# An adapter layer in float32 on one core: the residual rows added by accumulating DMAs, under a new order of steps

## The chip, the cores and the metric

The kernel runs on one core of a Trainium2 chip. The metric is the device time of one execution in microseconds (us); the time of a version is the median of its runs. Besides, one execution is recorded by the profiler. Its span is the time from the first to the last instruction.

## The reference

For each of 64 samples, x is 64 channels by 1024. The kernel computes a grouped convolution with a context term, then a dense layer with low-rank terms, and adds x itself at the end:

```python
out = conv1d(x, weight, groups=4, K=9, pad=4) + (c @ c_weight.T)[:, :, None] + bias[None, :, None]
A_eff = einsum('bn,nri->bri', gate, lora_A);  B_eff = einsum('bn,nor->bor', gate, lora_B)
y = out @ kernel + ffn_bias
y += B_eff (A_eff out)  +  lora_B_shared (lora_A_shared out)     # per batch of 8 samples
return x + y                                                     # float32, 64 x 64 x 1024
```

## The kernel before

The work is split into 16 "pairs" of four samples (256 rows of 1024). For each pair p there are four groups g of channels, and four output blocks b of 128 x 512: b = 2 * half of the rows + half of the columns. All products are made of float32 values split into a high and a low part (steps named ...hi and ...lo), with three matmuls in place of one.

*Convolution.* `xload` brings a group of x. From pair 3 on, `xohi`/`xolo` split its odd columns and `convo` multiplies them into PSUM; `evmid` moves that to SBUF with the context term added, either on ScalarE ("a", four activations) or on VectorE ("v", one addition). `xdiff` forms differences of columns, `xdhi`/`xdlo` split them, `convd` multiplies them, `evac` adds both parts, and `turned` transposes the result on VectorE. In the first three pairs `xhi`, `xlo` and `conv` do this directly.

*Dense layer.* From pair 1 on, a scheme with 7 products in place of 8 is used: `asum` (GpSimd) forms sums of input blocks, `yhi`/`ylo` split them, and `prod p j` is 12 matmuls into one of the accumulators a, d, c, b. Pair 0 uses `plain`. `keep p j` copies an accumulator to SBUF on ScalarE, `xsum` adds the accumulator b to the first copy (call the result X), `ysum` adds two further copies (call it Y). `lora`, `axlow`, `axsum`, `axhi`, `axlo` make the low-rank factor, and `delta p b` adds its product and the bias to the accumulator of block b.

*End of a block.* `rload p b` brings the 128 x 512 rows of x into a buffer r (SyncE's DMA queue; there are four such buffers). `radd` adds X to it for blocks 1, 2 and 3, `yadd` adds Y for block 3, `total` adds the accumulator on VectorE, and `store` writes r out from ScalarE's DMA queue:

```python
    def radd(p, b, eng="p"):
        r = res[p, b]
        engs[eng].tensor_tensor(r, r, cop[p, "x"], ALU.add)
```

In the opening, weights (`wload`) are loaded, the shared low-rank term is folded into them (`fmm`, `fadd`), they are combined (`wsum`) and split (`whi`, `wlo`), and the gated factors are made by `lload`, `mix`, `mixout`, `mixput` and read back by `aload` and `bload`. `busy` are matmuls on constants ahead of any data.

*Order.* A long string, ORDER, lists every step with its arguments; a last letter names the engine where there is a choice (v VectorE, p GpSimd, a ScalarE). The steps are emitted in this order, and each engine and each DMA queue runs its instructions in the order of emission, since a dependency without a semaphore ties each instruction to the one before it on its engine. The string was written ahead of time; nothing is planned at run time. A buffer of a pool is given out when the step that makes it is emitted, and waits for the last use of the buffer's former content.

Of the kernel before, what the change touches and what calls it, by code (L numbers as in the profile page):

```python
# [10 lines left out]
ALU = mybir.AluOpType  # L11
# [39 lines left out]
small 1, warm, twload 1, busy 29, twload 0, cwload, gload, ctload, cwide, cmul, thi 2, small 0, thi 0, tlo 0 v,  # L51
xload 0 0, xhi 0 0, tlo 2 p, xload 0 1, xlo 0 0 v, conv 0 0, twsum v, xhi 0 1, xlo 0 1 v, conv 0 1, sbload 1,
sbhi 1, csum, evac 0 0 v, turned 0 0, xload 0 2, xhi 0 2, xload 0 3, saload 0, sblo 1 p, xlo 0 2 p, evac 0 1 v,
turned 0 1, saload 1, gmask, xhi 0 3, conv 0 2, xlo 0 3 p, sahi 1, conv 0 3, sahi 0, salo 0 v, fmm 0 1,
sbload 0, sbhi 0, fmm 1 1, wload 1 0, evac 0 2 a, xload 1 0, sblo 0 v, fmm 1 0, salo 1 v, xload 1 1, xhi 1 0,
xhi 1 1, xlo 1 1 p, xlo 1 0 v, turned 0 2, yhi 0 0, ylo 0 0 p, wload 0 1, fadd 0 1, evac 0 3 a, fadd 1 0,
conv 1 0, whi 7 0, fmm 4 0, turned 0 3, xload 1 2, xhi 1 2, wlo 7 0 v, fmm 3 0, wload 1 1, conv 1 1, fadd 1 1,
wload 4 0, fmm 0 0, whi 0 1, wload 0 0, fadd 0 0, evac 1 0 a, plain 0 1 0, fadd 4 0, xlo 1 2 p, turned 1 0,
whi 0 0, wlo 0 1 p, fmm 2 1, fmm 2 0, yhi 0 7, evac 1 1 a, conv 1 2, fmm 5 0, wload 2 1, wload 2 0, fadd 2 0,
wlo 0 0 p, plain 0 0 0, xload 1 3, fadd 2 1, wload 5 0, xhi 1 3, fmm 4 1, xlo 1 3 p, plain 0 0 1, whi 0 2,  # L60
ylo 0 7 v, fadd 5 0, plain 0 3 0, whi 7 1, yhi 0 4, wload 3 0, fadd 3 0, whi 0 3, wload 5 1, fmm 3 1, conv 1 3,
turned 1 1, wlo 7 1 v, wload 3 1, xload 2 0, plain 0 1 1, fadd 3 1, whi 7 2, evac 1 2 v, wlo 7 2 p, wload 4 1,
wlo 0 3 p, wlo 0 2 v, lload 0 6, plain 0 2 0, whi 7 3, plain 0 3 1, fadd 4 1, wload 7 1, turned 1 2, whi 1 1,
plain 0 1 2, lload 0 7, xhi 2 0, plain 0 0 2, ylo 0 4 v, plain 0 3 2, xlo 2 0 v, plain 0 2 1, fmm 5 1,
evac 1 3 a, xload 3 0, wlo 7 3 v, plain 0 2 2, turned 1 3, whi 1 0, yhi 0 1, ylo 0 1 v, fadd 5 1, whi 6 1,
conv 2 0, wload 7 0, thi 1, xdiff 3 0 0 v, wload 6 0, evac 2 0 a, lload 1 5, wlo 1 0 p, fmm 7 0, fadd 7 0,
plain 0 2 3, plain 0 0 3, fmm 6 0, lload 0 2, plain 0 3 3, plain 0 1 3, fadd 6 0, lload 0 5, whi 6 0, asum 1 2,
yhi 1 2, lload 0 0, yhi 1 0, plain 0 0 4, plain 0 2 4, wsum 2 2 v, whi 2 2, lload 1 1, wlo 1 1 p, plain 0 0 5,
fmm 6 1, tlo 1 v, plain 0 2 5, rload 0 2, wlo 6 0 v, wsum 2 1 v, wsum 2 3 v, whi 1 2, wlo 1 2 v, plain 0 1 4,
whi 2 1, asum 1 3, whi 1 3, wlo 1 3 p, xload 2 2, wload 6 1, fadd 6 1, xload 2 1, whi 6 2, lload 0 1, xhi 2 2,  # L70
plain 0 3 4, lload 0 4, plain 0 2 6, lload 1 0, lload 0 3, wsum 2 0 v, fmm 7 1, plain 0 2 7, xload 2 3,
plain 0 0 6, fadd 7 1, whi 6 3, total 0 2, lload 1 6, mix 0 0, mixout 0 0 a, wlo 6 2 v, xhi 2 1, wlo 6 3 v,
wlo 6 1 v, wsum 3 2 v, xlo 2 2 v, mix 0 3, mixout 0 3 a, mix 0 2, mixout 0 2 a, wsum 3 0 v, wsum 5 0 v,
mixput 0 0, whi 2 3, mix 0 1, wsum 3 1 v, mix 1 0, mixput 0 3, mixout 0 1 a, xdiff 3 0 1 p, wsum 4 0 v,
conv 2 2, wlo 2 2 v, whi 2 0, wlo 2 0 v, ylo 1 2 v, plain 0 1 5, wsum 5 1 v, rload 0 0, wsum 5 2 v, wsum 4 2 v,
xlo 2 1 v, plain 0 0 7, mixput 0 1, ylo 1 0 p, mixput 0 2, wlo 2 1 v, prod 1 0, plain 0 1 6, wsum 3 3 v,
wsum 5 3 v, rload 0 1, plain 0 3 5, wsum 4 3 v, bihi, whi 3 2, keep 1 0, plain 0 1 7, lload 1 3, wsum 4 1 v,
plain 0 3 6, mixout 1 0 a, lload 1 7, mix 1 3, aload 0, whi 5 3, yhi 1 3, rload 0 3, lload 1 2, ylo 1 3 v,
mixout 1 3 a, total 0 1, lora 0, mix 1 1, turned 2 0, lora 1, whi 5 0, bilo, xohi 3 0, lload 1 4, mix 1 2,
whi 4 2, wlo 4 2 v, mixout 1 1 a, xolo 3 0 v, whi 3 0, wlo 3 0 v, wlo 3 2 v, yhi 1 1, ylo 1 1 v, mixout 1 2 a,  # L80
asum 1 5, total 0 0, whi 4 1, conv 2 1, axlow 1, axsum 1, xload 3 2, wlo 4 1 p, wlo 2 3 v, whi 4 0,
plain 0 3 7, axlow 0, axsum 0, mixput 1 0, mixput 1 3, wlo 4 0 v, xhi 2 3, xlo 2 3 v, wlo 5 3 v, axhi 1,
prod 1 1, biput 0, axlo 1, whi 3 3, asum 1 6, yhi 1 6, wlo 3 3 v, mixput 1 1, evac 2 1 a, turned 2 1, aload 1,
mixput 1 2, total 0 3, evac 2 2 v, turned 2 2, bload 0 0, whi 3 1, axhi 0, prod 1 2, keep 1 2, conv 2 3,
bhi 0 0, biput 1, yhi 2 0, evac 2 3 a, blo 0 0 v, axlo 0, yhi 1 4, bload 0 1, wlo 3 1 p, prod 1 3, ylo 2 0 v,
delta 0 0 1, total 0 0 1, bhi 0 1, blo 0 1 v, ylo 1 6 p, prod 1 6, whi 4 3, delta 0 3 1, wlo 4 3 v, store 0 0,
ylo 1 4 p, turned 2 3, delta 0 2 1, total 0 3 1, xdhi 3 0, convo 3 0, yhi 1 5, whi 5 1, ylo 1 5 v, xdlo 3 0 v,
delta 1 0, total 0 2 1, xload 3 1, keep 1 3, prod 1 4, evmid 3 0 a, store 0 3, xohi 3 1, xdiff 3 1 0 v,
xdiff 3 1 1 p, wlo 5 1 p, delta 0 1 1, total 0 1 1, wlo 5 0 v, xolo 3 1 p, convd 3 0, evac 3 0, turned 3 0,
asum 2 3, rload 1 0, convo 3 1, yhi 2 1, xdhi 3 1, xdlo 3 1 v, prod 2 0, whi 5 2, store 0 2, delta 1 2,  # L90
xload 3 3, keep 2 0, wlo 5 2 p, yhi 2 3, prod 1 5, total 1 0, xohi 3 3, xolo 3 3 v, asum 2 2, xdiff 3 2 0 p,
store 1 0, convo 3 3, evmid 3 1 a, xdiff 3 2 1 p, convd 3 1, ylo 2 3 v, prod 2 3, rload 1 3, delta 1 1,
ylo 2 1 v, xsum 1, asum 2 5, prod 2 1, xdhi 3 2, evac 3 1, turned 3 1, rload 1 2, radd 1 2 v, xdlo 3 2 v,
xdiff 3 3 0 v, delta 1 3, xohi 3 2, xdiff 3 3 1 p, yhi 2 5, xolo 3 2 v, ylo 2 5 p, yhi 2 2, ylo 2 2 v,
evmid 3 3 a, radd 1 3 v, convo 3 2, total 1 2, store 0 1, evmid 3 2 a, convd 3 2, xdhi 3 3, xdlo 3 3 v,
rload 1 1, radd 1 1 v, bload 1 0, lora 2, axlow 2, asum 2 6, prod 2 2, total 1 1, convd 3 3, evac 3 2,
turned 3 2, axsum 2, xload 4 0, xohi 4 0, xolo 4 0 p, bhi 1 0, yhi 2 4, ylo 2 4 v, axhi 2, prod 2 5, keep 2 3,
yhi 3 0, ysum 1 p, xdiff 4 0 0 v, xdiff 4 0 1 v, prod 2 4, store 1 1, xload 4 1, xohi 4 1, xolo 4 1 p,
yadd 1 v, blo 1 0 v, xdhi 4 0, axlo 2, delta 2 0, yhi 2 6, evac 3 3, keep 2 2, xdlo 4 0 v, convo 4 0,
turned 3 3, convd 4 0, rload 2 0, evmid 4 0 a, total 1 3, total 2 0, ylo 3 0 v, lora 3, xdiff 4 1 0 v,  # L100
xdiff 4 1 1 p, asum 3 3, yhi 3 3, prod 3 0, convo 4 1, ylo 3 3 v, evac 4 0, turned 4 0, xdhi 4 1, xload 4 3,
xohi 4 3, xdlo 4 1 v, asum 3 2, xolo 4 3 v, yhi 3 2, ylo 2 6 v, xload 4 2, xdiff 4 2 0 p, store 1 2,
xdiff 4 2 1 p, xohi 4 2, prod 3 3, yhi 3 1, bload 1 1, evmid 4 1 a, delta 2 2, ylo 3 2 v, xolo 4 2 v, asum 3 5,
store 2 0, convd 4 1, xdhi 4 2, xsum 2, convo 4 2, evmid 4 2 a, evac 4 1, xdlo 4 2 v, rload 2 2, radd 2 2 p,
total 2 2, xdiff 4 3 0 v, xdiff 4 3 1 p, prod 2 6, turned 4 1, yhi 3 4, bhi 1 1, convd 4 2, evac 4 2, keep 3 0,
prod 3 2, ylo 3 1 v, rload 2 3, radd 2 3 v, ysum 2 v, convo 4 3, yadd 2 v, xdhi 4 3, xdlo 4 3 v, ylo 3 4 v,
aload 2, prod 3 1, convd 4 3, turned 4 2, blo 1 1 p, xload 5 0, yhi 3 5, xohi 5 0, keep 3 2, asum 3 6,
keep 3 3, xload 5 1, xohi 5 1, delta 2 3, prod 3 4, delta 2 1, xdiff 5 0 0 p, xdiff 5 0 1 v, axlow 3,
ylo 3 5 p, evmid 4 3 a, total 2 3, prod 3 5, store 2 3, xolo 5 0 p, rload 2 1, yhi 3 6, radd 2 1 p, rload 3 0,
axsum 3, evac 4 3, axhi 3, turned 4 3, yhi 4 0, axlo 3, delta 3 0, xload 5 2, xdhi 5 0, store 1 3, xdlo 5 0 v,  # L110
convd 5 0, convo 5 0, ylo 3 6 v, bload 2 0, ylo 4 0 v, xdiff 5 1 0 v, xdiff 5 1 1 p, total 2 1, prod 3 6,
evmid 5 0 a, prod 4 0, asum 4 3, yhi 4 3, evac 5 0, xsum 3, yhi 4 4, ylo 4 3 p, delta 3 3, delta 3 2,
total 3 0, ylo 4 4 v, lora 4, xolo 5 1 p, xdhi 5 1, xdlo 5 1 v, store 3 0, yhi 4 1, ylo 4 1 v, xohi 5 2,
convo 5 1, keep 4 0, bhi 2 0, prod 4 1, rload 3 3, asum 4 2, yhi 4 2, radd 3 3 v, turned 5 0, xdiff 5 2 0 p,
ysum 3 v, evmid 5 1 a, xdiff 5 2 1 v, ylo 4 2 v, delta 3 1, xolo 5 2 p, rload 3 1, radd 3 1 p, blo 2 0 v,
# [702 lines left out]
```

## Time and profile before

| | us |
|---|---|
| median of three runs | 448.88 |
| lowest and highest run | 448.42, 450.63 |
| profiled execution | 447.48 |
| its span | 445.7 |
| TensorE (PE) busy | 438.3 |
| VectorE (DVE) busy | 391.3 |
| ScalarE (ACT) busy | 251.2 |
| GpSimd (POOL) busy | 234.5 |

The profile's page lists each engine's busy time as a share of the span. A group of instructions is given by line, engine, operation, and tiles as out<-in; then come the busy time, the mean nanoseconds of one, and the idle time of the engine just before them with what ended it. SP is SyncE, and a "q" behind an engine's name means its DMA or instruction queue. DMA moved 67.05 MB; SyncE's queue took 38.9% of the DMA engines' time and ScalarE's 10.2%.

### The profile page before, as it was taken

To read this page: it belongs to the slowest core of one execution; us is meant where nothing else is said; L and a number is where in the kernel's file an instruction comes from. 1 tells how busy PE (TensorE), PEld (TensorE's weight loads), DVE (VectorE), ACT (ScalarE), POOL (GpSimd) and SP (SyncE) were. 2 spreads that over 40 slices of the span, in tenths; PEclk is the share of its full clock that TensorE was granted. 3 is DMA by queue.
4 is the path that set the end of the run, shared out by engine and by line. 5 is a ranking of instruction groups with operands and counts; after the bars stand their busy time and mean duration, and the time that the engine had idled before them with its cause. 6 is when DMAs were issued, how large, how long until landed. Compare 5 with 4: busy or idle time off the path is not lost.

```text
span 445.7 us, 7717 instructions
## 1 busy us (share of the span) xinstructions
PE 438.3 (98%) x2557; PEld 358.7 (80%) x2557; DVE 391.3 (88%) x615; ACT 251.2 (56%) x639; POOL 234.5 (53%) x202
## 2 busy tenths in 40 slices
PE   8999999999999999999999999999999999999996
PEld 7677658888888888888878888888888888888884
DVE  5998979899899899889899899899798989887783
ACT  5877468556655566446555655646554745654440
POOL 3766024754747653555444445464656475467543
PEclk9999999999999999999999999999999999999999
DMA  8999582461625463534345453443536354262243
GB/s 229 300 280 308 147 251 66 142 186 49 186 82 158 136 190 110 170 120 136 97 139 147 151 182 91 119 142 90 175 98 186 95 169 151 72 222 90 91 150 118
DMA packets 52488, 67.05 MB, mean 150 GB/s; under 512 B 6112, under 2 KB 34016, under 8 KB 52448
## 3 DMA queue, kind: packets, MB, share of 16 engines
q1 hardware_dynamic: 42512, 49.83, 38.9%
q10 hardware_dynamic: 9936, 16.73, 10.2%
q8 instruction: 20, 0.33, 0.3%
q14 instruction: 20, 0.16, 0.1%
HBM read 47.65 MB, written 18.87 MB: 149 GB/s over the span
## 4 chain that ended last, share of the span: by engine, by line
PE 91%; DMA 4%; DVE 2%; issue 1%; SPq 0%; ACT 0%; ACTq 0%; DVEq 0%
PE mm_a L592 19%; PE mm_d L592 18%; PE mm_c L592 17%; PE mm_b L592 9%; PE cv L346 8%; PE cm L346 4%; PE axp L602 3%; PE cv L318 2%; DMA wr<-in_dram 2%; PE mx L528 2%; PE mm_a L580 1%; PE mm_c L580 1%; DMA ls<-in_dram 1%; DMA ctt<-in_dram 1%; PE mm_d L580 1%; PE mm_a L660 1%
## 5 line engine op out<-in xcount | busy, mean ns | idle before, releaser
L592 PE MATMUL mm_a<-wh,y 128*128 128x512 f32 x240 | 79.6, 392 | 0.0
L592 PE MATMUL mm_d<-wh,y 128*128 128x512 f32 x240 | 79.2, 391 | 0.0
L592 PE MATMUL mm_c<-wh,y 128*128 128x512 f32 x240 | 79.1, 391 | 0.0
L364 ACT ACTIVATE md<-cm,cadd 128x64 f32<-128x64 f32 x208 | 48.2, 315 | 44.8 <-PE cm L346 41.1
L326 POOL TENSOR_TENSOR xf<-xt 128x256 f32<-128x256 f32 x45 | 33.3, 747 | 49.4 <-DVE xd L270 39.4
L265 ACT CAST xd<-xf 128x512 fp32r<-128x512 f32 x52 | 32.5, 626 | 44.9 <-PE cv L346 20.7
L265 ACT CAST y<-s 128x512 fp32r<-128x512 f32 x60 | 37.2, 624 | 30.5 <-POOL s L412 15.3
L592 PEld LDWEIGHTS mm_a<-wh,y 128*128 128x128 f32 x240 | 45.1, 188 | 9.9 <-issue 0.4
L592 PEld LDWEIGHTS mm_d<-wh,y 128*128 128x128 f32 x240 | 45.1, 188 | 9.2 <-issue 0.2
L592 PEld LDWEIGHTS mm_c<-wh,y 128*128 128x128 f32 x240 | 45.1, 188 | 9.1 <-ACT c L636 0.2
L387 DVE STREAM_TRANSPOSE z<-v 128x512 f32<-128x512 f32 x64 | 45.4, 709 | 3.2 <-PE axp L602 1.9
L592 PE MATMUL mm_a<-wl,y 128*128 128x512 f32 x120 | 46.9, 391 | 0.0
L592 PE MATMUL mm_c<-wl,y 128*128 128x512 f32 x120 | 46.8, 390 | 0.0
L592 PE MATMUL mm_d<-wl,y 128*128 128x512 f32 x120 | 46.8, 390 | 0.0
L346 PE MATMUL cv<-xd,th 128*128 128x256 f32 x208 | 45.7, 282 | 0.4 <-DVE xd L270 0.4
L378 DVE TENSOR_TENSOR v<-cv,md 128x512 f32<-128x512 f32 x52 | 35.7, 686 | 7.7 <-PE cv L346 2.5
L270 DVE TENSOR_TENSOR xd<-xf,xd 128x512 fp32r<-128x512 f32 x41 | 34.5, 842 | 7.6 <-ACT xd L265 7.4
L270 DVE TENSOR_TENSOR y<-s,y 128x512 fp32r<-128x512 f32 x49 | 38.2, 782 | 3.0 <-ACT y L265 2.7
L592 PE MATMUL mm_b<-wh,y 128*128 128x512 f32 x120 | 39.6, 391 | 0.0
L346 PEld LDWEIGHTS cv<-xd,th 128*128 128x128 f32 x208 | 35.5, 188 | 2.4 <-DVE xd L270 0.6
L265 ACT CAST y<-z 128x512 fp32r<-128x512 f32 x49 | 30.6, 625 | 11.8 <-DVE c L641 4.5
L326 DVE TENSOR_TENSOR xf<-xt 128x256 f32<-128x256 f32 x59 | 33.7, 587 | 0.2
(132 smaller groups left out, 1008.2 us busy)
## 6 DMA issues: line engine op xcount, KB each, us to landing
xt<-in_dram SPq DMA_DIRECT2D x64, 258.0 KB, 3.2
r<-in_dram SPq DMA_DIRECT2D x64, 256.0 KB, 3.5
out_dram<-r ACTq DMA_DIRECT2D x63, 256.0 KB, 2.6
ls<-in_dram SPq DMA_DIRECT2D x16, 256.0 KB, 4.6
br<-eff SPq DMA_DIRECT2D x48, 64.0 KB, 2.8
wr<-in_dram SPq DMA_DIRECT2D x16, 176.0 KB, 4.2
eff<-ls SPq DMA_DIRECT2D x16, 128.0 KB, 2.7
wr<-in_dram SPq DMA_DIRECT2D x16, 80.0 KB, 3.9
```

Source lines behind the costliest of these rows:

```text
L265: nc.scalar.copy(dst, src)
L270: engs[eng].tensor_tensor(dst, src, f32(hi), ALU.subtract)
L318: nc.tensor.matmul(ps, a[:, 2 * kt, g, :], b[:, :, kt:kt + P], start=(n == 0), stop=(n == 5))
L326: engs[eng].tensor_tensor(xdf[p, g][:, e], m, odd(p, g), ALU.subtract)
L346: nc.tensor.matmul(ps, a[:, w, g, :], b, start=(n == 0), stop=(n == 2))
L364: nc.scalar.activation(t[:, n], cpm[p, g][:, n], ACTF.Identity, bias=c[:, n:n + 1])
L378: nc.vector.tensor_tensor(v.rearrange("p n (i e) -> p e n i", e=2), cps.pop((p, g)), mid.pop((p, g)).unsqueeze(1).to_broadcast([P, 2, 4, H ...
L387: nc.vector.transpose(z[:, :, :, :, gg, :], vs.pop((p, g)).rearrange("p m j -> p (m j)"))
L528: nc.tensor.matmul(mps[w, j][n * e:n * e + n], gm.rearrange("p b i -> p (b i)"), lraw[w, 2 * j + e], start=True, stop=True)
L580: nc.tensor.matmul(acc[p, BLOCKS[b]], m[:, kk, :], n, start=(k == 0 and q == 0), stop=(k == 7 and q == 2))
L592: nc.tensor.matmul(ps, a[:, k, :], b[bb, k], start=s, stop=(k == HK - 1 and q == 2), skip_group_check=not first)
L602: nc.tensor.matmul(axp[q * R:q * R + R, p % 2, :], a[:, k, :], zs[p, hf][:, k, :], start=k < 2, stop=k >= 6)
```

## The change

For pairs 1 to 14 (numbered from 0) and blocks 1, 2 and 3, x is no longer loaded ahead and added by an engine. `total` now adds the accumulator to X (blocks 1 and 2) or to Y (block 3) and writes the sum to a new r buffer. A new step `racc` issues a DMA from GpSimd's queue that reads the rows of x and adds them to r in place; `store` follows it. For block 3 a new step `xysum` first adds X to Y. Block 0 of every pair, and pairs 0 and 15, go on as before.

The order of all steps is new, from the first step on. Among its differences: `rload` 64 to 22, `radd` 45 to 3, `yadd` 15 to 1, `racc` 42 and `xysum` 14 new (11 on VectorE, 3 on GpSimd). `evmid` is on ScalarE 26 times instead of 52, else on VectorE; `evac` of the first pairs on ScalarE 4 times instead of 8. On GpSimd are 56 `xdiff` instead of 45, 21 `xdlo` instead of 11, 6 `ysum` instead of 2. The number of matmul steps of each kind is the same.

```diff
 ORDER = """
-small 1, warm, twload 1, busy 29, twload 0, cwload, gload, ctload, cwide, cmul, thi 2, small 0, thi 0, tlo 0 v,
+cwload, xload 0 0, twload 1, warm, twload 0, gload, gmask, busy 29, ctload, thi 2, tlo 2 p, cwide, cmul,
...
+yhi 0 1, lload 0 4, whi 1 3, whi 6 3, lload 0 5, wlo 7 3 v, wlo 1 0 p, plain 0 2 4, wsum 2 3 p, plain 0 1 3,
...
+lload 0 7, plain 0 0 5, plain 0 3 4, whi 6 2, wlo 6 2 v, rload 0 2, total 0 2, mix 0 3, xhi 2 1, mixout 0 3 a,
+whi 2 2, lload 0 1, rload 0 1, wsum 5 0 p, mix 0 0, mixout 0 0 a, yhi 1 0, xload 3 0, turned 1 3, asum 1 2,
...
+xdiff 5 0 0 p, xdiff 5 0 1 p, ylo 4 0 v, prod 3 1, store 1 2, xysum 2 v, convo 5 0, total 2 3, xload 5 1,
+racc 2 3, convd 4 3, store 1 1, racc 2 2, xohi 5 1, axhi 3, xolo 5 1 p, evmid 5 0 v, keep 3 3, xdhi 5 0,
+xdlo 5 0 p, rload 3 0, prod 3 5, prod 3 4, ysum 3 v, convd 5 0, yhi 3 6, ylo 3 6 v, prod 3 6, xdiff 5 1 0 p,
...
+store 12 1, prod 13 4, xdiff 15 0 0 p, prod 13 6, evmid 14 3 v, store 12 3, xdiff 15 0 1 p, ysum 13 v,
...
+ysum 15 p, yadd 15 v, total 15 3, prod 15 6, totalh 15 1 0, rload 15 0, total 15 0, store 15 3, store 15 0,
+rload 15 2, radd 15 2 v, storeh 15 1 0, prod 15 4, delta 15 2, total 15 2, store 15 2, totalh 15 1 1,
+storeh 15 1 1
 """
...
+    def xysum(p, eng="p"):
+        t = cop[p, 2]
+        engs[eng].tensor_tensor(t, t, cop[p, "x"], ALU.add)

     def total(p, b, of=0):
-        r = res[p, b]
-        nc.vector.tensor_tensor(r, acc[p, (BLOCKS[b], b)[of]], r, ALU.add)
+        a = acc[p, (BLOCKS[b], b)[of]]
+        if (p, b) in res:
+            r = res[p, b]
+            nc.vector.tensor_tensor(r, a, r, ALU.add)
+        else:
+            r = res[p, b] = slot("r", f"r{b}_{p}")
+            nc.vector.tensor_tensor(r, a, cop[p, 2 if b == 3 else "x"], ALU.add)
+
+    def racc(p, b):
+        nc.gpsimd.dma_start(res[p, b], xrow(x, p, b), accum_op=ALU.add)
```

## The prediction

> **What bounds the kernel now.** I read the engine shares and the chain of waits first, then what TensorE waited for, then the windows, and the groups by line last.
>
> ```profile
> span 445.7 us, 7717 instructions
> PE 438.3 (98%) x2557; PEld 358.7 (80%) x2557; DVE 391.3 (88%) x615; ACT 251.2 (56%) x639; POOL 234.5 (53%) x202
> ...
> PE 91%; DMA 4%; DVE 2%; issue 1%; SPq 0%; ACT 0%; ACTq 0%; DVEq 0%
> ```
>
> TensorE carries 91% of the chain. A busy PE need not be at its peak, so I looked at its pitch: in the chain every product of 12 matmuls takes 2.72 to 2.78 us, early and late. The list of PE's waits (whole: three more of 0.4 us and less) and two of the windows show that nothing holds it up.
>
> ```profile
> PE idle L701 <- DVE axt L695: 1.2, 1, 1.2
> PE cv L318 <- POOL xsl L270: 0.6, 1, 0.6
> PE cv L346 <- DVE xd L270: 0.4, 1, 0.4
> ```
>
> ```profile
> 100.00:120.00 20.00, 20.00 (x129) 16.85 (x128) 18.56 (x31) 12.16 (x33) 11.16 (x11) 1.00 0.40 120
> ...
> 240.00:260.00 20.00, 20.00 (x132) 16.92 (x131) 17.73 (x30) 10.50 (x29) 8.80 (x9) 1.00 0.38 124
> ```
>
> A wait line ends in us in total, times, longest. The windows' columns are PE, PEld, DVE, ACT and POOL busy, granted clock (1.00), DMA share and GB/s. From 80 to 440 us PE is busy 19.57 to 20.00 of every 20.
>
> The floor, from the chain's pieces: 105 products at 2.74 = 287.7; 32 plain steps at 0.70 = 22.4; 12 early convolutions at 1.42 = 17.0; 52 pairs of convo (0.36) and convd (0.70) = 55.1; 16 lora at 1.01 = 16.2; 64 deltas at 0.235 = 15.0; 8 mixes at 0.95 = 7.6; 16 fmm at 0.23 = 3.7. Sum 424.7. The first convolution starts at 7.47, the last matmul ends at 441.67: 434.2. So only 9.5 us are not matmul pitch, 3 of them between 7.5 and 20 us and most of the rest switches between kinds of matmul. Whatever the change takes off VectorE, ScalarE or SyncE can return no more than part of this; the matmuls stay the same in number and shape.
>
> **The change part by part.** The rows for it, from the groups by line, from SyncE's waits and from the DMA issues (KB each, us to landing):
>
> ```profile
> L649 DVE TENSOR_TENSOR r<-r,c 128x512 f32<-128x512 f32 x36 | 26.8, 746 | 1.7 <-DMA r<-in_dram 1.6
> ...
> L653 DVE TENSOR_TENSOR r<-r,c 128x512 f32<-128x512 f32 x14 | 10.5, 751 | 0.1
> ...
> L364 ACT ACTIVATE md<-cm,cadd 128x64 f32<-128x64 f32 x208 | 48.2, 315 | 44.8 <-PE cm L346 41.1 <-DVE r L666 2.0 <-PE mm_b L592 0.9
> ```
>
> ```profile
> SPq L632 <- DMA out_dram<-r: 75.4, 21, 10.2
> ```
>
> ```profile
> r<-in_dram SPq DMA_DIRECT2D x64, 256.0 KB, 3.5
> out_dram<-r ACTq DMA_DIRECT2D x63, 256.0 KB, 2.6
> ```
>
> *VectorE.* radd falls from 36 to 1 (35 x 0.746 = 26.1 us) and yadd from 14 to 1 (9.8); xysum adds 11 (priced by the yadd row: 8.3). Of what the new order reassigns, evmid adds 26 (priced by cadd, the same shape out of PSUM, 0.414: 10.8) and four evac 2.7; 11 xdiff (0.587) and 10 xdlo (0.842) leave with 14.9; the rest nets to -6.5. Sum -35.5: 391 to about 356 us. *ScalarE.* 26 evmid of four activations (26 x 4 x 0.315 = 32.8) and four evac (5.9) go: 251 to about 214, the overlap of its instructions counted. *SyncE.* 42 loads of r go, with about 0.54 us of issue each, and with them most of the 75 us for which SP held its queue until a store had landed. All three are gains beside a PE that did not wait for them: worth 0. What hides them is the matmul stream; if that cover went, VectorE at 356 would still be under 424.7.
>
> *GpSimd arithmetic.* Seven radd and one yadd leave (11.1); 11 xdiff at 0.747, 10 xdlo at 1.398, four ysum and three xysum at 1.34 and smaller ones come: net +29, so 234 to 263 us. A rule of the Trainium skill speaks against this (page "SBUF — State Buffer", "Who interferes with whom"): a VectorE instruction with two SBUF inputs contends with a GpSimd one that reads SBUF, and the later fully blocks. The rows show less: two-input 128x512 operations take 746 to 842 ns against 680 with one input in PSUM, so 0.07 to 0.16 us each while GpSimd is at 53%. By the row, 29 us more of GpSimd costs VectorE some 3 us; by the rule, up to 29. I take the row; by either, VectorE stays below PE.
>
> *The 42 accumulating DMAs.* No row shows one. Their issue on GpSimd is bounded below by ScalarE's issue of a store (0.55 us); above I take 2.6. That upper end is also the page's fixed cost ("DMA: Bandwidth & Descriptors", "Anatomy of one DMA": about 2.0 us plus bytes/436e3, an estimate of 2.6 for 256 KB), as if GpSimd were held for all of it. I take 1.0, nearer the row[...]: 42 us, GpSimd at 305 (68%). For the landing that rule gives 2.6, but here a plain load of the same rows took 3.5. The accumulate also reads its target, so the ends are 2.6 and 7.0; I take 3.5, which makes 4.5 from issue to sum.
>
> *The waits that it adds.* racc sits in GpSimd's order behind total; xdiff, xdlo, xolo and asum queue behind it. The store sits in ScalarE's order behind the landing; casts queue behind that. total itself now takes the r buffer, so VectorE, not SP, waits for an older store. To see the room, I gave each step of the order the matmul time of the steps ahead of it (the floor's prices). From delta to the first arithmetic on GpSimd behind its racc there are mostly 4 to 20 us, against about 0.7 for total and 1.0 for the issue: covered. From racc to its store most have 3 us or more against 4.5, and the cases that I followed (store 12 1, store 7 3) have no cast due on ScalarE before it is free. One place is late: total 2 3 waits for store 1 2 (115.8 + 2.6 landing), then 0.7, two raccs (2.0), xolo (0.9), xdlo (1.4): 123.4, where convd 5 0 is due at 122.3: +1.1. Ends: 0 and 8 us over the whole run.
>
> *The opening.* Its loads are asked for earlier. At 37 us of matmul time (44.1 us in the trace) the loads that the mix steps need end at 11.11 and 11.37 MB of the queue before, and at 11.89 and 12.42 MB after. Adding the windows' GB/s, 11.11 MB had passed by 40.4 us, 3.7 early; 12.42 MB pass at 44.8, and the second mix is now due at 45.1, with the semaphore of the landing still to come. conv 0 2 needs 2.05 MB instead of 1.59 at 10.4 us, where 2.27 had passed by 10. I take +1.5 (from 0 to 4).
>
> *The end.* Before, the last work is two halves of 0.42 us and two 128 KB stores (2.1 to 2.2 us). Now a whole total (0.69), a half (0.42) and a 256 KB store (2.6) follow the last matmul: +0.3 us for the addition, +0.1 for the store.
>
> Sum: 445.7 + 1.5 + 0.4 + 1.1 = 448.7 of span, +1.8 around it (the profiled run took 447.48) = 450.5. The median shown, 448.88, is 1.4 above that run; so 451.9 as a median, +0.7%.
>
> **The rivals.** (1) GpSimd becomes the bound. In the order's stretch from 240 to 260 us of matmul time stand 23.2 us of its work with five raccs at 1.0 us (before: at most 16.9 in any such stretch). At 2.6 us it is 31, 11 behind, and the next stretch (13.8 plus 3.2) gives back only 3. Some 8 us reach PE through xdlo and asum: about 459. For: no price is measured. Against: 53% busy now, and long distances. (2) Everything stays covered, the opening too: 448.5 to 449. For: PE saw only 3 us of waits with VectorE at 88%. (3) Faster: VectorE is busy 18.99 of 20 us from 20 to 40, next to the bound there, and the new opening gives GpSimd several of its low halves, and more of the work to an idle engine. If that closes the 3 us of gaps before 20 us and the loads still arrive, 447.48 - 3 + 1.4 = 445.9. It decides if PE's first 24 plain matmuls come without gaps. Against: the loads are the limit there (DMA share 0.96). (4) That x is not added by the DMA's own adder but split into more packets would show as a landing near 7 us, and leads to (1).
>
> **How the numbers follow.** The measurement tells about 0.5% from no change, that is 446.6 to 451.1. The case of the sum has 0.45 (own range 449 to 456; 0.33 slower, 0.12 same), rival 1 and 4 0.20 (455 to 468), rival 2 0.22 (0.20 same, 0.02 slower), rival 3 0.13 (0.12 faster). Slower 0.55, same 0.33, faster 0.12. The range from 446.5 to 462 leaves out most of rival 3 and the upper part of rival 1.
>
> **What would show it.** PE: products still at 2.72 to 2.78 in the chain, gaps near 44 us "<-DMA ls" and in the window of pair 5's first convd; VectorE near 356, ScalarE near 214, GpSimd near 263 plus issues. A landing of r<-in_dram on GpSimd's queue near 3.5 to 4.5 us. If the landing is above 7 us, or PE waits on GpSimd's xd and s by several us in total, rival 1 is right. If PE's last matmul starts before 439 us, I am wrong on the opening.

## The result, and the profile after

The changed kernel takes 473.43 us in the median of four runs (472.29 to 474.51), the kernel before on the same chip 448.65 (448.07 to 450.63): a ratio of 1.0544, 95% interval 1.0503 to 1.0585. It is slower by 24 us. The prediction had the side right ("slower" at 0.55), but 451.9 us and a range up to 462.

The shares and the chain of the profile after:

```profile
span 471.5 us, 7600 instructions
...
PE 449.0 (95%) x2557; PEld 359.4 (76%) x2557; DVE 396.6 (84%) x579; ACT 224.7 (48%) x518; POOL 298.3 (63%) x269
...
PE 67%; DVE 17%; DMA 5%; issue 4%; ACT 2%; POOL 2%; SPq 1%; ACTq 0%; DVEq 0%; POOLq 0%
```

TensorE has the same 2557 matmuls and is busy 10.7 us longer for them. It is also idle 15.1 us longer, 6.3 of these in the first 60 us. VectorE issues 36 instructions fewer and is busy 5.3 us longer. Its share of the chain has gone from 2% to 17%. From 60 us on, TensorE's listed waits sum to 8.9 us, all but 0.2 for VectorE's results. Three of these lines, and one of the opening (pf):

```profile
PE cm L341 <- DVE xo L265: 2.7, 3, 1.6
PE cm L341 <- DVE md L361: 2.2, 1, 2.2
...
PE pf L470 <- POOL sa L265: 1.7, 1, 1.7
...
PE cv L341 <- DVE v L373: 1.4, 2, 1.1
```

The rows of the change itself, from the groups by line, from GpSimd's waits and from the answer on the line of `racc`:

```profile
L673 POOL DMA_DIRECT2D r<-in_dram x42 | 41.8, 1031 | 30.4 <-DVE r L670 29.6
...
POOL r L673 <- DVE r L670: 29.6, 13, 6.9
...
DMA to landing us min/median/max: 4.0/4.9/7.0
```

An issue takes 1.03 us of GpSimd, the DMA lands 4.9 us after it, and 13 times GpSimd stood at `racc` until `total` had run, 29.6 us together.

The row that matters most is neither of these. These are the answers on the tile y, for VectorE alone, first of the kernel before, then of the kernel after (duration in ns: min/median/max):

```profile
L270 DVE TENSOR_TENSOR y<-s,y x49: 650/684/1773, 50.9 to 435.5; 128x512 fp32r<-128x512 f32 x49
```

```profile
L265 DVE TENSOR_TENSOR y<-s,y x46: 651/692/3804, 59.9 to 456.5; 128x512 fp32r<-128x512 f32 x46
```

The median is the undisturbed duration in both; a few operations are held. Before, the longest is 1.77 us; after, it is 3.80. I added up over all of VectorE's operations with two inputs in SBUF what each took beyond its undisturbed 0.68 us (0.41 for the half-size ones): 45.6 us before, 78.1 after. None of them took over 2 us before, twelve did after. Operations with an input in PSUM are as they were (`total` of products: group medians of 681 to 692 ns before, 679 to 692 after). The sum moves by up to 0.4 us with what is taken as undisturbed for the odd shapes.

The longest of them can be followed in the chain of waits (start us, us, what), with the TensorE clock in the windows behind it (PE, PEld, DVE, ACT, POOL busy, granted clock, DMA share, GB/s):

```profile
336.41 0.67 DVE xf L321 x2
337.08 3.72 DVE y L265
340.80 0.60 DVE r L667
341.40 0.61 DVE v L373
...
342.04 0.71 DVE z L382
342.75 2.14 DVE xf L321 x2
344.89 0.35 DVE md L361
...
345.28 0.62 PE cm L341 x3
345.90 4.34 PE mm_a L587 x12
```

```profile
343.00:345.20 2.20, 0.10 (x1) 0.00 (x0) 2.20 (x3) 0.20 (x1) 1.61 (x2) 1.00 0.00 1
...
346.00:348.00 2.00, 2.00 (x7) 1.54 (x6) 1.30 (x3) 1.21 (x6) 0.00 (x0) 0.65 0.79 232
348.00:349.00 1.00, 1.00 (x4) 0.81 (x3) 0.00 (x0) 0.60 (x2) 0.00 (x0) 0.50 0.27 102
349.00:350.20 1.20, 1.20 (x5) 0.98 (x4) 0.00 (x0) 0.00 (x0) 0.00 (x0) 0.59 0.48 181
```

One `ylo` on VectorE is held for 3.1 us; `evac` and the `evmid` behind it come late; TensorE stands for 1.1 and then 2.2 us. In the three windows behind that, its granted clock is 0.65, 0.50 and 0.59, and the product there takes 4.34 us; the other products of this stretch, at 1.00, take 2.80. The timeline shows what stood beside that `ylo`: the issue of a `racc` and two operations of GpSimd right behind it.

```profile
336.71 0.96 POOL L673 DMA_DIRECT2D r<-in_dram  x1 [3.94 <-DVE r L670]
...
337.00 3.80 DVE L265 TENSOR_TENSOR y<-s,y 128x512 fp32r<-128x512 f32 x1
...
337.32 1.67 POOL L407 TENSOR_TENSOR s<-s,z 128x512 f32<-128x512 f32 x1
...
338.57 1.68 POOL L265 TENSOR_TENSOR xd<-xf,xd 128x512 fp32r<-128x512 f32 x1
```

### The profile page after: what moved, and what is told of

It is laid out like the page before. It is cut to its first block, busy times and chain, and to the rows that moved or that the text cites. A ratio compares the mean times of both kernels' runs of the same rounds, so it can differ in the third digit from the quotient of the medians.

```text
span 471.5 us, 7600 instructions
## 1 busy us (share of the span) xinstructions
PE 449.0 (95%) x2557; PEld 359.4 (76%) x2557; DVE 396.6 (84%) x579; ACT 224.7 (48%) x518; POOL 298.3 (63%) x269
## 4 chain that ended last, share of the span: by engine, by line
PE 67%; DVE 17%; DMA 5%; issue 4%; ACT 2%; POOL 2%; SPq 1%; ACTq 0%; DVEq 0%; POOLq 0%
PE mm_c L587 15%; PE mm_a L587 13%; PE mm_d L587 13%; PE mm_b L587 6%; PE cv L341 6%; DVE y L265 4%; PE cm L341 3%; DVE xo L265 2%; PE axp L597 2%; DVE xf L321 2%; DVE xd L265 2%; PE mx L523 2%; DMA wr<-in_dram 1%; DVE r L670 1%; DMA xt<-in_dram 1%
## 5 line engine op out<-in xcount | busy, mean ns | idle before, releaser
L587 PE MATMUL mm_a<-wh,y 128*128 128x512 f32 x240 | 81.9, 402 | 0.1
L587 PE MATMUL mm_d<-wh,y 128*128 128x512 f32 x240 | 80.7, 398 | 1.1 <-DVE y L265 1.1
L587 PE MATMUL mm_c<-wh,y 128*128 128x512 f32 x240 | 80.5, 396 | 0.4 <-DVE y L265 0.4
L260 ACT CAST xd<-xf 128x512 fp32r<-128x512 f32 x52 | 32.5, 625 | 73.4 <-PE cv L341 34.5
L321 POOL TENSOR_TENSOR xf<-xt 128x256 f32<-128x256 f32 x56 | 44.2, 811 | 33.6 <-DVE xd L265 24.3
L673 POOL DMA_DIRECT2D r<-in_dram x42 | 41.8, 1031 | 30.4 <-DVE r L670 29.6
L265 DVE TENSOR_TENSOR y<-s,y 128x512 fp32r<-128x512 f32 x46 | 48.0, 1046 | 8.9 <-ACT y L260 7.9
L587 PE MATMUL mm_a<-wl,y 128*128 128x512 f32 x120 | 48.1, 401 | 0.0
L265 POOL TENSOR_TENSOR xd<-xf,xd 128x512 fp32r<-128x512 f32 x21 | 31.5, 1498 | 18.5 <-ACT xd L260 18.2
L265 DVE TENSOR_TENSOR y<-z,y 128x512 fp32r<-128x512 f32 x41 | 39.2, 958 | 1.9 <-ACT y L260 1.7
```

Of the source, the lines that this page charges most:

```text
L260: nc.scalar.copy(dst, src)
L265: engs[eng].tensor_tensor(dst, src, f32(hi), ALU.subtract)
L321: engs[eng].tensor_tensor(xdf[p, g][:, e], m, odd(p, g), ALU.subtract)
L587: nc.tensor.matmul(ps, a[:, k, :], b[bb, k], start=s, stop=(k == HK - 1 and q == 2), skip_group_check=not first)
L673: nc.gpsimd.dma_start(res[p, b], xrow(x, p, b), accum_op=ALU.add)
```

## The experiments

Each was timed against the kernel before on the same chip; the ratio is to that. Names with a_ start from the changed kernel, names with b_ from the kernel before, and those with g_ join the opening of one order to the rest of the other. "Excess" is the sum over VectorE's two-input operations as above.

| kernel | median us | ratio, 95% | DVE busy | excess |
|---|---|---|---|---|
| before | 448.65 | | 391.3 | 45.6 |
| after | 473.43 | 1.0544 (1.0503 to 1.0585) | 396.6 | 78.1 |
| a_noracc | 460.94 | 1.0277 (1.0252 to 1.0302) | 375.6 | 56.1 |
| a_scratch | 463.38 | 1.0328 (1.0299 to 1.0358) | 382.6 | 63.5 |
| a_wait | 467.85 | 1.0433 (1.0390 to 1.0476) | 386.5 | 67.2 |
| a_wait2 | 468.25 | 1.0422 (1.0388 to 1.0456) | 384.6 | 65.5 |
| a_accdram | 472.96 | 1.0532 (1.0506 to 1.0559) | 395.4 | 76.5 |
| a_spacer | 476.20 | 1.0602 (1.0577 to 1.0626) | 395.9 | 76.5 |
| a_late | 488.77 | 1.0877 (1.0844 to 1.0911) | 386.8 | 67.7 |
| a_move | 467.31 | 1.0423 (1.0392 to 1.0455) | 387.6 | 58.1 |
| b_misalign | 454.56 | 1.0124 (1.0087 to 1.0161) | 392.6 | 47.0 |
| a_align | 474.64 | 1.0564 (1.0524 to 1.0604) | 397.3 | 78.1 |
| a_place | 469.76 | 1.0464 (1.0423 to 1.0505) | 397.1 | 78.9 |
| g_openafter | 461.52 | 1.0277 (1.0237 to 1.0316) | 395.7 | 52.8 |
| g_openbefore | 465.71 | 1.0368 (1.0333 to 1.0404) | 397.8 | 77.2 |
| g_repair | 466.81 | 1.0391 (1.0348 to 1.0435) | 393.8 | 72.0 |
| g_move | 458.16 | 1.0213 (1.0178 to 1.0248) | 389.1 | 56.1 |
| b_racc | 508.09 | 1.1318 (1.1285 to 1.1352) | 407.4 | 82.4 |

### The order without the DMAs, and then the DMAs piece by piece

*a_noracc*: `racc` does nothing; x is not added in its 42 blocks.

```diff
     def racc(p, b):
-        nc.gpsimd.dma_start(res[p, b], xrow(x, p, b), accum_op=ALU.add)
+        pass
```

> The changed kernel without the 42 accumulating DMAs: total and store stay, so x is not added for those blocks. Theory A (the accumulating DMAs on GpSimd stretch VectorE's two-input operations and hold GpSimd's order; the new opening costs some 6.7 us of its own): 473.4 less the 18 us of gaps behind the opening, 455 (452 to 458), and VectorE's y<-s,y falls from 1046 to about 850 ns. Theory B (the new order itself is slow, whatever GpSimd issues): 466 or more.

460.94 us. So about half of the loss, 12 us, is in the new order without any DMA of the change, where the prediction had 1.9 (opening and end). From 60 us on, TensorE's listed waits are 0.9 us here and 8.9 in the change.

*a_scratch*: the rows of x go to scratch in HBM instead, by a plain DMA in the same place (x is not added). It waits for nothing.

```diff
-        nc.gpsimd.dma_start(res[p, b], xrow(x, p, b), accum_op=ALU.add)
+        t = dram.tile([P, HN], F32, tag=f"sc{b}_{p}", name=f"sc{b}_{p}")
+        nc.gpsimd.dma_start(t, xrow(x, p, b))
```

> In the changed kernel each accumulating DMA is a plain copy of the same rows of x to a scratch in HBM, issued at the same place of GpSimd's order; nothing waits for it and it waits for no total (x is not added for those blocks). The issue stays (1.0 us each), the wait for total and the wait for the landing go. Theory A1 (the issue with arithmetic right behind it stretches VectorE): 466 to 472, two-input operations over 2 us still there. Theory A2 (the waits do it): as without the DMAs, 453 to 458.

463.38 us, 2.4 above a_noracc: 42 plain issues with their traffic.

*a_wait*: the same, but the source is the summed block r (x is not added). GpSimd waits for `total`, as in the change; no store waits for a landing.

```diff
+        nc.gpsimd.dma_start(t, res[p, b])
```

> In the changed kernel each accumulating DMA is a plain copy of the summed block to a scratch in HBM, from GpSimd's queue: it is issued at the same place and still waits for total, but the store no longer waits for a landing (x is not added for those blocks). If GpSimd's wait for total is what costs (29.6 us in all), this is near 470 and the one without that wait near 456; if the landing at 4.9 us is what costs, this is near 458 and the changed kernel's extra comes from ScalarE behind its stores.

467.85 us, 4.5 more. The waits of GpSimd at this line are 28.7 us in 15 times, those of the change. So the wait that the prediction called covered costs some 4.5 us (the four runs lie between 466.27 and 470.23). Not all of it need be GpSimd's standing: the excess rises by 3.7 us too. 5.6 us are left between this kernel and the change.

*b_racc*: the order of before, with each `racc` right behind its `total`, its store 16 steps later, and `xysum` on VectorE.

> The order of before with the same replacement alone: for pairs 1 to 14, blocks 1 to 3, no load, radd or yadd; total, the accumulating DMA right behind it, the store 16 steps later, xysum on VectorE behind xsum and ysum. Everything else in the order of before, so VectorE loses about 25 us of work and GpSimd gets 42 issues. Theory A: the issues and landings cost here too, 455 to 465. Theory B (only the new order is slow): 446 to 450.

508.09 us, with GpSimd held by `total` for 108.6 us in 35 times. The DMA can't simply be put into the old order. The new one, costly as it is, moves most of these waits out of the way.

### Why the order without the DMAs costs 12 us: where y and w lie

In the records, the products' matmuls follow each other at 227 ns in the kernel before (mean of all without a gap: 228.4) and at 233 ns after (233.0), from the first product to the last, in a_noracc too. b_racc, with the old order, has 228.7. From 80 us on the granted clock is 1.00 in both. What differs is the place of tiles in SBUF: a pool lays its tags out in the order of their first use, which the new order changes. In the built programs the weight tiles `wh` and `wl` (the moving operand) start at byte 64 modulo 256 before and at 32 after; the tiles y (the stationary operand) at 64 in both.

*a_align* and *b_misalign* add two unused pads of 32 bytes to the pool.

```diff
+        if "pad" not in used:
+            used["pad"] = work.tile([P, 8], F32, tag="pad", name="pad", bufs=1)
```

> The changed kernel with two unused pads of 32 bytes in the work pool, so that the weight tiles wh and wl (the moving operand of every product) start at multiples of 64 bytes, as they do before the change; after the change they start 32 bytes past one. Theory 'placement of the weights sets the matmul pitch': products back at 227 to 228 ns a matmul (233 after), about 1540 x 4.6 ns = 7 us less, 466 to 467. Theory 'the pitch is the clock or the busier memory': pitch stays at 233, 473.

> The kernel before with the same two pads, which put wh and wl 32 bytes past a multiple of 64 and leave every other tile's start, modulo 64, as it was. Nothing else changes. Theory 'placement': pitch 232 to 233 ns, +7 us, about 456. Theory 'clock or busier memory': 448.8.

b_misalign: pitch 233.0, 454.56 us. Two unused pads cost the old kernel 1.24%, 5.6 us (0.87 to 1.61%): placing is a cause. (1356 matmuls read wh or wl: 105 products of 12 and 32 plain steps of three; at 4.6 ns that is 6.2 us. The 1540 of the expectation counted others too.) a_align: pitch still 233.2, 474.64 us: the theory that w alone must be at a multiple of 64 is wrong. The pads had moved y as well: y is at 128 modulo 256 in both, w at 64 in a_align and at 96 in b_misalign. That left the place of w relative to y.

*micro* measures this alone: groups of 24 matmuls on resting data at 16 placings of y and w. (It then puts VectorE beside GpSimd, but GpSimd's issues did not run where they were meant to stand; micro2 below has that part.)

> No part of the reference is computed (the output is zeros): the two disputed costs by themselves. First TensorE alone, groups of 24 products (128x512, the three terms of the split as in the kernel) at 16 placings of the stationary y and the moving w. Theory 'relative placement': where y and w start at the same byte modulo 128 (64/64, 0/0, 32/32, 96/96, 64/192, 64/320) the pitch is 227 ns, at the other nine 233 ns. Theory 'both must sit at 64 modulo 128': only 64/64, 64/192 and 64/320 at 227. Theory 'it is the other engines' traffic': all 16 alike. Then VectorE's additions of two SBUF tiles beside GpSimd doing nothing, subtractions in a row, DMA issues alone, an issue followed by one subtraction, by two, and accumulating DMAs followed by two. Theory 'behind a DMA issue VectorE is held through GpSimd's next one or two operations': 0.68 us beside nothing and beside issues alone, 0.9 to 1.4 beside subtractions in a row, over 2 us at an issue followed by subtractions. Theory 'only GpSimd's share of time counts': beside issue and subtraction no longer than beside subtractions in a row.

The timeline of TensorE (start us, us; a line with x24 is one group; the tile's name has only the place of y). In order, the placings y/w are 32/32, 96/96, 32/96, 64/0, 0/32, 32/0, 96/32 and, at 98.27, 64/192:

```profile
59.43 5.63 PE L95 MATMUL y32w<-big 128*128 128x512 f32 x24
64.89 5.64 PE L95 MATMUL y96w<-big 128*128 128x512 f32 x24
70.37 5.66 PE L95 MATMUL y32w<-big 128*128 128x512 f32 x24
75.88 5.76 PE L95 MATMUL y64w<-big 128*128 128x512 f32 x24
81.47 5.76 PE L95 MATMUL y0w<-big 128*128 128x512 f32 x24
87.07 5.76 PE L95 MATMUL y32w<-big 128*128 128x512 f32 x24
92.67 5.76 PE L95 MATMUL y96w<-big 128*128 128x512 f32 x24
98.27 16.83 PE L95 MATMUL y64w<-big 128*128 128x512 f32 x72
```

From start to start, 24 matmuls take 5.46 and 5.48 us where y and w start at the same byte (after some ten matmuls the records show 226.7 ns each), 5.51 where w lies 64 further, and 5.59 to 5.60 (233 ns) where it lies 32 or 192 or 224 further. The other placings agree, with one miss: at 128 further (64/192), which the expectation had among the fast, it is 232 ns, while 256 further is fast. So it is the distance modulo 256, not 128. DMA traffic was going on in the first groups and not in the last; it makes no difference.

*a_place* puts both at 64 modulo 256 in the changed kernel, by pads of 32 and 224 bytes.

> The changed kernel with two unused pads (32 and 224 bytes) in the work pool, so that the weight tiles and the y tiles start at the same byte modulo 256 again, as before the change; nothing else differs. Theory 'relative placement of y and w': the products' pitch falls from 233 to 228 ns. In time, if it adds up with the rest: 1540 x 4.6 ns = 7 us, 466; if VectorE and GpSimd hold the kernel in places and the faster TensorE only waits for them: 470 to 472. If the pitch stays at 233, the theory is wrong: 473.

The pitch falls to 228.3 ns, as the theory has it, and the time to 469.76 us. Of the 5.6 us that placing costs the old kernel, 3.6 come back here; the ratio's interval, 1.0423 to 1.0505, just meets that of the change (1.0503 to 1.0585). Why not all of it comes back is not shown. TensorE's idle time is no longer than in the change (22.2 and 22.5 us in the profiled executions), so the missing part was not seen as a longer wait.

### The opening and the rest of the order

*g_openafter*: the new order up to `prod 2 3`, then the old one; no accumulating DMA at all. (It has y at 128 and w at 64, thus the slow pitch of 233.2; its expectation took the place of w alone for the cause.)

> The changed order up to prod 2 3, the order of before from there on, no accumulating DMA at all, and the pads that put the weight tiles at multiples of 64. Theory 'opening': +6.5 us alone, 455. If the opening's delay is made up later by the order of before (its slack), 449 to 450.

461.52 us. Less the 5.6 us of placing, if the two simply add, the new opening costs 6.8 us. The ratio is that of a_noracc: as far as these two show, the rest of the new order costs nothing by itself. (a_noracc lacks the work on x in 42 blocks, so VectorE is busy 375.6 us there and 395.7 here.) The windows of the first 60 us show the opening, first before, then after (sums over six windows of 10 us):

```profile
sum 60.00, PE 57.45 PEld 41.60 DVE 52.08 ACT 37.83 POOL 27.72; mean PE 9.57 PEld 6.93 DVE 8.68 ACT 6.31 POOL 4.62
```

```profile
10.00:20.00 10.00, 7.02 (x28) 4.71 (x27) 7.83 (x11) 4.58 (x8) 7.85 (x7) 1.00 0.97 272
20.00:30.00 10.00, 8.29 (x33) 5.58 (x33) 9.74 (x16) 6.74 (x12) 9.18 (x8) 1.00 0.85 253
30.00:40.00 10.00, 8.38 (x36) 6.13 (x35) 6.89 (x11) 5.09 (x10) 8.18 (x7) 1.00 0.83 244
...
sum 60.00, PE 51.20 PEld 34.88 DVE 45.36 ACT 30.23 POOL 40.10; mean PE 8.53 PEld 5.81 DVE 7.56 ACT 5.04 POOL 6.68
```

TensorE is busy 6.3 us less. It stands between 10 and 40 us, not at the mix steps near 44 us which the prediction watched, while GpSimd is busy 25 of these 30 us (20 before). The chain of waits there goes through a load and then four low halves that GpSimd makes, in 1.26 to 1.31 us each where VectorE takes 0.69 (the first of the four is in the chain with its last part only). From 18.8 us on it goes through SyncE's issues and loads, those of weights (wr) among them, and a low half of VectorE (xsl) that takes 1.67 us. The last line is a plain step (mm_d) that waited 1.6 us for VectorE's addition to a weight:

```profile
8.72 4.67 DMA sar<-in_dram
14.04 0.78 POOL sb L265
14.89 1.26 POOL sa L265
16.24 1.29 POOL xs L265
17.53 1.28 POOL xsl L265
21.66 2.34 DMA wr<-in_dram
24.01 1.67 DVE xsl L265
25.71 4.55 DMA bia<-in_dram
32.58 3.90 DMA wr<-in_dram
37.76 0.97 PE mm_d L575 x3
```

Between 18.8 and 21.6 us stand short issues of SyncE, and the first of them is an `xload` that was held for 0.5 us until GpSimd's `xlo` was done with its input. Loads of weights are queued behind it. Of TensorE's waits in this stretch 2.6 us end on GpSimd's results and 4.2 on VectorE's. So slow low halves and late loads both have a part. How much is due to each, and which step of the new opening would have to go back, was not tried.

*g_openbefore*: the old opening, then the new order with its DMAs; y and w both at 64, pitch 228.4.

> The order of before up to prod 2 3 and the changed order with its 42 accumulating DMAs from there on; the weight tiles are at multiples of 64 here. Theory 'the change costs opening + placement + DMAs': opening (6.5) and pitch (7) both gone, DMAs stay: 448.8 + 12.5 = 461. Theory 'the new order of the rest costs, not the opening': 467 or more.

465.71 us, 16.5 above the kernel before, not 12.5: with opening and placing right, the DMAs and their order cost 4 us more than they add on top of them. The causes overlap; the three alone are 6.8 + 5.6 + 16.5 = 28.9 us, together 24.4.

### The last 5 us: issue time, landing, or VectorE?

*a_wait2*: two plain DMAs of r to scratch for each `racc`, 84 issues at 0.55 us (x is not added).

> The changed kernel with each accumulating DMA replaced by two plain GpSimd DMAs of the summed block to scratch in HBM (x is not added in these blocks): the wait for total stays, the issue time is 2 x 0.56 = 1.12 us as the accumulating one's 1.03, and no store waits for a landing. Theory 'the last 5.6 us are issue time on GpSimd': 473. Theory 'they are the landing and the store that waits for it': 468, as with one plain DMA (467.9).

468.25 us, as with one, and the excess is not larger either (65.5 and 67.2). More issue time on GpSimd did not cost by itself here, though part of it took the place of waiting: the wait for `total` fell from 28.7 to 19.8 us. This pointed to the landing.

*a_accdram*: the accumulating DMA turned round.

```diff
-        nc.gpsimd.dma_start(res[p, b], xrow(x, p, b), accum_op=ALU.add)
+        t = dram.tile([P, HN], F32, tag=f"sc{b}_{p}", name=f"sc{b}_{p}")
+        nc.gpsimd.dma_start(t, res[p, b], accum_op=ALU.add)
```

> The changed kernel with each accumulating DMA turned round: it adds the summed block onto scratch in HBM (x is not added in these blocks). Issue of the accumulating kind and the wait for total stay; no store waits for a landing. Theory 'the accumulating issue shuts VectorE out': 472 to 474, VectorE busy near 396. Theory 'landing': 468, as with one or two plain DMAs.

472.96 us with VectorE at 395.4: the whole loss with no store that waits for a landing. Landing is out. (The DMA reads r here, and could hold its buffer longer; but VectorE never waits for that in this trace.) In the change, too, ScalarE waited for one only once, 2.9 us. The issue is 0.93 us here, against 0.56 of the plain one in a_wait.

*micro2*: the second half of micro again, in a fixed order.

> No part of the reference is computed (the output is zeros): VectorE's additions of two SBUF tiles beside GpSimd in a fixed order: subtractions in a row; four plain DMA issues; four accumulating issues; plain issue and two subtractions, four times; accumulating issue and two subtractions; accumulating issue, tiny issue and two subtractions. Theory 'shut-out': 0.69 us alone and beside issues of either kind with no arithmetic behind them; 1.6 to 1.7 beside subtractions in a row; the addition beside an issue and the subtraction behind it about 1.8 with the plain issue and 2.2 to 2.8 with the accumulating one; with the tiny issue between, near 1.7 to 1.9. If the issue itself blocks, the row of four issues shows it.

The windows of VectorE's additions alone (us, busy and number, clock, DMA share, GB/s). In order: beside subtractions in a row; four plain issues; four accumulating issues; four times a plain issue and two subtractions; four times an accumulating issue and two; four times an accumulating issue, a tiny issue and two.

```profile
17.48:32.45 14.97, 14.69 (x9) 1.00 1.02 381
34.44:43.11 8.67, 8.29 (x12) 1.00 0.96 333
43.65:52.33 8.68, 8.30 (x12) 1.00 1.09 313
53.58:67.41 13.83, 13.59 (x8) 1.00 0.67 226
73.75:89.15 15.40, 15.15 (x8) 1.00 0.48 68
97.67:114.66 16.99, 16.74 (x8) 1.00 0.45 62
```

An issue with no arithmetic behind it costs VectorE nothing, of either kind: 0.69 us an addition. Beside subtractions in a row each addition takes 1.63 us: it is let in once between two of them. With an issue ahead of two subtractions, VectorE is held during a part of the issue as well (not from its start: an addition that began 0.05 us after an accumulating issue took 0.68 us). Beyond 8 x 1.63 = 13.06, four plain issues add 0.13 us each, four accumulating ones 0.52 each, and accumulating with tiny ones 0.92 a pair. In single additions: 1.63 us beside subtractions, 1.68 to 1.81 at a plain issue, 2.09 to 2.19 at an accumulating one, and 2.13 to 2.70 with the tiny one. So the tiny issue does not free VectorE, against the expectation: it lengthens the hold.

*a_spacer*: that tiny DMA behind each `racc` in the kernel.

> The changed kernel with a second, tiny GpSimd DMA (512 B, to scratch) right behind each accumulating one, so that what is queued behind the accumulating issue is another issue and not arithmetic; 42 issues more. Theory 'shut-out': VectorE's busy time falls from 396 to about 385 and the time to 468 to 470. Theory 'landing' or 'GpSimd's time': 473 or more, as GpSimd has more to do.

476.20 us, VectorE at 395.9. The idea for a remedy was wrong, as micro2 shows. But the longer hold of micro2 does not show in the kernel's sum: the longest hold is 5.40 us instead of 3.80, and the excess is 76.5 against 78.1. Why this kernel is 2.8 us slower is open.

*g_repair*: the same in g_openbefore's order.

> The order of before up to prod 2 3 and the changed order from there, with the accumulating DMAs and the tiny DMA behind each; y and w start at the same byte modulo 256 here. Theory 'opening, placement and shut-out are causes of their own': 465.7 less some 4 us, 461 to 462. It does not reach the kernel before (449), since issues, and the wait for total, stay. If shut-out is not a cause: 466.

466.81 us (g_openbefore 465.71): no gain either, with an excess of 72.0 against 77.2.

*a_move*: in the trace of the change, GpSimd's next arithmetic follows within 50 ns at 23 of the 42 issues, and VectorE's operations beside these are over by 32.0 us (a_accdram 26.9; a_wait, 18 places, 16.7). The same held operations can be found in a_wait and in the change, longer by the difference of the issues: 2380 and 2772 ns, 3182 and 3593, 3399 and 3804. a_move takes these 23 steps from GpSimd.

```diff
-racc 4 2, ... xdiff 6 2 1 p
+racc 4 2, ... xdiff 6 2 1 v
-racc 8 1, ... asum 10 3
+racc 8 1, ... asum 10 3 v
```

> The changed kernel with the 23 GpSimd steps that follow an accumulating issue within 50 ns (xdiff, xolo, xdlo, asum, ylo, ysum) given to VectorE; places in the order unchanged. Theory 'VectorE held behind the issue is what costs': about 23 x 0.69 = 16 us of work come to VectorE, most of the 32 us of holding go, its busy time falls to 380 to 388, and the time to 467 to 470 in spite of the added instructions. If holding is not what costs: VectorE has 16 us more to do and the time is 473 to 476.

*g_move*: the same in g_openbefore's order, 24 steps.

> The same move, made at the 24 such places of the order with the opening and the placing of before (465.7 us). Theory 'holding': 460 to 462, and still above the kernel before, since the wait for total stays. If holding is not what costs: 466 or more.

467.31 and 458.16 us. VectorE has 23 and 24 instructions more and is busy 9 us less, its excess falls from 78.1 to 58.1 and from 77.2 to 56.1, and the kernels gain 6.1 and 7.6 us. From 60 us on, TensorE's listed waits fall from 8.9 us to 4.8 in a_move. With micro2 and a_accdram, this shows the cause of this part: arithmetic close behind an issue, and VectorE shut out for it and for part of the issue. How much of the 6.1 and 7.6 us is the hold alone stays open, since the moved steps also no longer stand behind GpSimd's wait for `total`, and no run moved as many steps from other places. g_move still is 9.7 us above the kernel before. There GpSimd still waits for `total` 14 times, 25.2 us.

*a_late*: each `racc` up to 20 steps later, but not within four steps of its store.

> The changed kernel with each accumulating DMA up to 20 steps later in the order (not within 4 steps of its store); nothing else moves. Theory 'GpSimd's wait for total costs': the 29.6 us in which GpSimd was held fall under 10, and 3 to 5 us come back, 469. Theory 'what costs is that issues and the arithmetic behind them shut VectorE out of its SBUF inputs': the wait goes, the time hardly moves, 472 to 474.

488.77 us, well off both. GpSimd's wait for `total` went (29.6 to 1.2 us), but in its place ScalarE stood at stores until the sum had landed, and the casts behind it were late. The waits of ScalarE:

```profile
ACT y L260 <- DMA r<-in_dram: 29.0, 7, 7.2
```

So this run says nothing on the price of the wait for `total`; it shows what the distance to the store was for. No version here beats the kernel before.

## Why the prediction was wrong, point by point

The sum had +3.0 us (opening 1.5, end 0.4, waits 1.1) where the runs have 24.4. The step that cost most, some half of the loss, is this: work put on GpSimd was weighed as busy time of an engine and dropped, because by that measure "VectorE stays below PE". The runs show that it holds single operations of VectorE and so delays their results. The rest is the opening, whose term was too small, and the pitch, which had no term.

*The floor and the relief: right.* It said that work taken off VectorE, ScalarE and SyncE is worth nothing beside a TensorE that does not wait. No run shows a gain from it. ScalarE fell to 224.7 us, not 214: the sum took `evmid` at its mean of 0.315 us, but the row's 48.2 us for 208 are 0.23 each, as these operations overlap.

*"The matmuls stay the same in number and shape": right, but the pitch was taken as given.* The sum had no term for it. It went from 228.4 to 233.0 ns because the new order changes where tiles lie; that costs 5.6 us in the old kernel, and 3.6 us in this one. No row of before shows the dependence; micro and b_misalign do.

*The opening: +1.5 (0 to 4) was mis-sized; alone it is 6.8 us.* The step that failed is the choice of what is due. The prediction followed the loads by the megabyte to the mix steps. The gaps are between 10 and 40 us, where the chain goes through low halves on GpSimd and then through loads of weights. It had weighed the low halves only as a gain, in rival 3.

*VectorE 391 to 356 us: wrong, 396.6.* The step is "By the row, 29 us more of GpSimd costs VectorE some 3 us; by the rule, up to 29. I take the row". The excess grew by 32.5 us (45.6 to 78.1), 10.5 of it without the DMAs (a_noracc, where GpSimd has 26.5 us more arithmetic) and 22 with them. Without the excess, VectorE's time fell by 27.2 us (345.7 to 318.5), not 35.5: the sum took operations away at the means of their rows, holds included. The rule of the Trainium skill ("SBUF — State Buffer", "Who interferes with whom") was right: the later instruction is blocked, not slowed (1.63 us against 0.69 in micro2). The row was misread. A mean of 782 ns looked like a slight slowing of all; the same row of before with its median of 684 and maximum of 1773 shows most at full speed and a few fully held.

*"By either, VectorE stays below PE": true and of no use.* VectorE at 84% bounds nothing by its share. A hold of 2 to 3.8 us is a delay of one result, and the distance from `ylo`, `xolo`, `xdlo`, `xdiff` and `evmid` to their matmuls is shorter than that in places.

*The issue, 1.0 us (0.55 to 2.6): right, 1.03 (median 0.96).* GpSimd's sum, 305 us, is 298 in the profile, and its arithmetic, 263, is 261 in a_noracc. But the sum took the issue as time of GpSimd alone. Its price is in VectorE: 5.1 us from a_wait to a_accdram, for 0.37 us more a piece, while the excess rises by 9.3.

*The landing, 3.5 us (2.6 to 7.0): mis-sized, 4.9 measured, within the bounds, and without effect:* a_accdram takes 472.96 us with no store that waits for one.

*The waits, "covered", +1.1: wrong.* GpSimd was held 29.6 us by `total`; by a_scratch and a_wait this costs about 4.5 us, the hold of VectorE that goes with it included. The rooms of 4 to 20 us were counted in matmul time from `delta`. But `total` runs when VectorE comes to it, and 13 times GpSimd stood for it, up to 6.9 us.

*The end, +0.4: 0.7 measured.* From the end of the last matmul to the end of the span it is 4.0 us before and 4.7 after.

*Rivals.* Rival 1, GpSimd as the bound, had 459 us, but from issues of 2.6 us; they are 1.03, twice the plain issue time costs nothing (a_wait2), and from 60 us on no listed wait of TensorE ends on GpSimd. Rivals 2 (all covered) and 3 (faster) fell with the result. Rival 4, longer landings, is out. The cause was in none of the rivals, though the rule that carries half of it stood in the text, with its price of up to 29 us of VectorE's time.

The sum as the runs have it, on the way from before to after: placing 5.6, opening 6.8, rest of the order 0 (together a_noracc's 12.3), plain issues 2.4, wait for `total` 4.5, accumulating kind of issue 5.1, landing 0.5: 24.8 us, for 24.4 by the ratio. The terms are differences of medians, some within the runs' spread of 2 to 4 us, and they overlap: in another sequence they would be other numbers.

## What to carry to other kernels

Before work is added to GpSimd, read min, median and max of VectorE's two-input operations, not their mean: in this kernel a median at full speed with a long tail meant that VectorE was shut out. Added GpSimd arithmetic, and DMA issues right ahead of it, lengthened the tail and delayed single results, whatever the shares of the engines. By micro2, an accumulating DMA belongs where GpSimd has no arithmetic to do just after it. And when an order is changed, compare the addresses of the matmul operands: first use lays out the pool.

## What the hardware showed unexpectedly

- The pitch of back-to-back float32r matmuls of 512 columns depends on the distance of the moving from the stationary tile modulo 256 bytes: 226.7 ns at 0, 229 at 64, 232 to 234 at 32, 96, 128, 192 and 224. 160 was not tried.
- In micro2, VectorE is held during part of a DMA issue on GpSimd if arithmetic stands behind the issue (0.52 us more for an accumulating one, 0.13 for a plain one), and not at all if none does (0.69 us). Why two plain issues in a row (1.1 us, a_wait2) cost the kernel no more than one stays open.
- An accumulating issue takes 0.93 to 1.03 us of GpSimd, a plain one 0.55 to 0.59, for the same 256 KB. They land after 4.7 to 4.9 us (a_accdram, the change) and 2.9 to 3.5 us (a_wait, a_scratch).
- After TensorE had stood for 1.1 and 2.2 us within 5 us, its granted clock was 0.65, 0.50 and 0.59 in the next windows. The product there took 1.5 us more than others, on top of 3.3 us of standing. That the standing is the reason was not tested.
